# Setup products in borrowed buffers, loads from two queues, and a new order of the late setup work: a two-layer graph network on one Trainium2 core

## The chip, the cores and the metric

The kernel runs on one core of a Trainium2 chip. The core has five engines that run side by side, each with its own queue of instructions in fixed order: TensorE (PE in the profile, with its weight loads as PEld), VectorE (DVE), ScalarE (ACT), GpSimd (POOL) and SyncE (SP), which here only issues DMAs. They wait for one another by semaphores. The metric is the device time of one execution in microseconds, from the first to the last instruction; lower is better.

## The reference

Sixty-four graphs of 256 nodes with 256 features pass through two layers, all in float32. Layer 0 is a graph attention network, layer 1 a transformer layer whose values depend on the kind of edge. Cut to what matters:

```python
def gat(h, adj, W, a):                       # twice, with W1, a1 and W2, a2
    Wh = h @ W
    e = leaky_relu(Wh @ a[:256] + swap(Wh @ a[256:]), 0.2)
    return softmax(where(adj > 0, e, -9e15), axis=1) @ Wh
def layer0(x):
    h = layernorm(x + gat(gat(x, adj, W1, a1), adj, W2, a2))
    return layernorm(h + relu(h @ w_ff1 + b_ff1) @ w_ff2 + b_ff2)
def layer1(s):                               # 8 heads of 32, R = 4 kinds of edge
    attn = softmax(q(s) @ k(s).T / sqrt(32))
    out = sum(attn * (adj == r) @ (s @ Wv[r] + bv[r]) for r in range(4))
    x = layernorm(s + out @ Wo + bo)
    return layernorm(x + gelu(x @ W1 + b1) @ W2 + b2)
```

## The kernel before

**Tiling.** The 64 graphs are taken in 32 pairs. One pair's features are a tile of 128 partitions by 4 by 256. `whole_way(pair)` is the whole course of a pair: `gat_layers` (lines L524, L540 and L553 are its matmuls), `feed_forward` of layer 0 (L677 is its first matrix, in block products of seven instead of eight, L708 its second), `attention` (L750 and L755 make queries, keys and values, L792 scores, L821 and L824 products with the values and the sums, L843 the output matrix), and `feed_forward` of layer 1. Matmul operands are float32; the trace shows each matmul as two records.

**Setup.** Ahead of all pairs, the kernel multiplies the two attention weight matrices of layer 0 together with the vectors `a1` and `a2` into one constant `w12` of 128 x 2 x 260. Four VectorE instructions (L111) form weighted row sums, four matmuls (L117) multiply, and two copies (L119) move the product out of PSUM. Its inputs lie in a pool `setup` of their own, which is closed afterwards; the pools `work` and `psum` are opened after it in the same memory. Adjacency of the first two pairs is loaded into a tile `v` of the pool `work`.

**Reliefs and block sums.** Some biases are folded into residuals, so other constants have to be corrected once. The generator `reliefs()` does it: narrow matmuls with one output column (L908) and a wide pair (L917) on TensorE, small subtractions on VectorE (L910, L919), and `block_sums` (L336), differences of quarters of a weight matrix that the block products need. A pair's first `feed_forward` waits for `relieved[0]`, its attention for `relieved[1]`, its last `feed_forward` for `relieved[2]`.

**The order.** The order of every engine's queue is made when the program is built, by a small planner (`run`, `put`). It keeps a clock for each engine, starting at `START`, and a due time for each event; the landing times of the constant loads are entered by hand (`landed`, `load(0, 11.0)`). Pieces of work for VectorE, ScalarE, GpSimd and SyncE are taken when they are ready, the lowest `rank` first. On TensorE, up to three pairs and the reliefs are generators that yield steps. Of the steps ready for at least `SLACK` microseconds it takes the first by a key; if none is ready for so long, the earliest. The order is then fixed on each engine: an instruction that waits holds up everything behind it on its engine. Two lines carry it:

```python
sure = [n for at, n in times if at <= now - SLACK]
g = going[min(sure, key=lambda n: ("ff" in (going[n][2] or ()) or alone.get("ff") is going[n][0], n))
```

The constant loads are issued by SyncE one after another. A load also waits until the load eight before it has landed, since eight semaphores are used in turn.

Of the kernel before, what the change touches and what calls it, by code (L numbers as in the profile page):

```python
# [10 lines left out]
F32 = mybir.dt.float32  # L11
# [4 lines left out]
ALU = mybir.AluOpType  # L16
AX = mybir.AxisListType

P = 128
# [5 lines left out]
SHIFT = 40.0  # L25
EVEN = 1e-37
HURRIED = 2
SLACK = 0.5
START = {"tensor": 12.0, "vector": 11.0, "scalar": 12.0, "gpsimd": 0.0, "sync": 40.0}


@with_exitstack
def two_layers(ctx: ExitStack, tc: tile.TileContext, t: dict, out: bass.AP, flag: bass.AP):
# [12 lines left out]
    nc = tc.nc  # L46
    B, N, D = out.shape
    NPAIR = B // 2
    KC = D // P
# [46 lines left out]
        nc.sync.dma_start(s, t[name])  # L96
        return s

    w12 = const.tile([P, KC, D + 4], F32, name="w12")
    with tc.tile_pool(name="setup", bufs=1) as setup, \
            tc.tile_pool(name="psetup", bufs=2, space=bass.MemoryType.PSUM) as psetup:
        w1T, a2 = weights("L0_gnn_W1T", setup), on_all("L0_gnn_a2", 2 * D, setup)
        right = setup.tile([P, KC, D + 4], F32, name="right")
        nc.sync.dma_start(right[:, :, :D], t["L0_gnn_W2"].rearrange("(c p) m -> p c m", p=P))
        nc.sync.dma_start(right[:, :, D + 2:], t["L0_gnn_a1c"])
        junk = setup.tile([P, D], F32, name="junk")
        for s in range(2):
            for c in range(KC):  # L110
                nc.vector.scalar_tensor_tensor(  # L111
                    junk, right[:, c, :D], 1.0, a2[:, s * D:(s + 1) * D], op0=ALU.mult, op1=ALU.mult,
                    accum_out=right[:, c, D + s:D + s + 1])
        for m in range(KC):
            pw = psetup.tile([P, 512], F32, name="pw")
            for c in range(KC):
                nc.tensor.matmul(pw[:, :D + 4], lhsT=w1T[:, c, m * P:(m + 1) * P], rhs=right[:, c],  # L117
                                 start=c == 0, stop=c == KC - 1)
            nc.vector.tensor_copy(w12[:, m], pw[:, :D + 4])  # L119
# [4 lines left out]

    def bank():
        return psum.tile([P, 512], F32, name="ps")

# [58 lines left out]
    def at_time(us):  # L186
        event = Event()
        event.time = us
        return event
# [19 lines left out]
    def run(besides, ways, together):  # L209
# [5 lines left out]
        while True:  # L215
# [22 lines left out]
            clock[engine] = now  # L238
            if engine == "tensor":
                sure = [n for at, n in times if at <= now - SLACK]  # L240
                g = going[min(sure, key=lambda n: ("ff" in (going[n][2] or ()) or alone.get("ff") is going[n][0], n))
                          if sure else min(times)[1]]
                alone.update((name, g[0]) for name in g[2] or ())
                takes("bank", g[3])
                for needs in g[4:]:
                    takes(needs)
                step = next(g[0], None)
                if step is None:
                    together -= g[0] is besides
# [235 lines left out]
    def gat_weights(y, at, at_home, ratio, there, to, b):  # L485
# [18 lines left out]
                k = 2 * b + j  # L504
                nc.scalar.activation(y[:, k, :at], y[:, k, :at], AF.Copy, scale=of["rs"][:, j:j + 1])
# [890 lines left out]
```

## Time and profile before

| | before |
|---|---|
| time, three runs | 3067.23, 3071.6 and 3072.2 us, median 3071.6 us |
| the profiled execution | 3069.0 us, span 3067.2 us |
| TensorE busy | 3008.9 us of the span, 98% |
| VectorE, ScalarE, GpSimd busy | 2565.5, 1805.6, 251.5 us |
| mean granted clock of TensorE | 0.991 of full speed |
| DMA | 205.75 MB, mean 67 GB/s |

In the first 80 us TensorE is busy for 60.42 us, in the 2900 us after that for all but some 20 us, and in the last 67.2 us for 48.43 us. All constants, 8 MB and more with the first pairs, come in over the first 50 us; from 20 to 30 us and from 46 to 53 us the DMA engines move about 350 GB/s. The granted clock of TensorE is half of full speed in several stretches of the first 70 us and again from about 3022 to 3031 us.

### The profile page before, as it was taken

How to read it: one execution, taken by the hardware profiler on the slowest of the kernel's cores; microseconds unless marked ns; L12 is line 12 of the kernel's file. 1: busy time of each engine (PE TensorE's matmuls, PEld its weight loads, DVE VectorE, ACT ScalarE, POOL GpSimd, SP SyncE). 2: the span in 40 equal slices, each digit the busy share in tenths (PEclk: the TensorE clock that was granted, in tenths of full speed). 3: DMA queues.
4: the chain of work that ended last, by engine and by line, in shares of the span. 5: the costliest groups of instructions: out<-in, count | busy, mean ns of one | idle time of the engine just before them, and what ended most of it. 6: DMA issues, size and time to landing. Idle time of an engine off the chain costs nothing. (4 is left out here: it accounts for less than half of the span.)

```text
span 3067.2 us, 52833 instructions
## 1 busy us (share of the span) xinstructions
PE 3008.9 (98%) x19138; PEld 2461.4 (80%) x19138; DVE 2565.5 (84%) x5993; ACT 1805.6 (59%) x4124; POOL 251.5 (8%) x518
## 2 busy tenths in 40 slices
PE   7999999999999999999999999999999999999997
PEld 6887778877888888888878888878888878888876
DVE  5798988789888898889798879898878898888875
ACT  3655666556565565665565665565755555755564
POOL 0000000100000001000011000011000010000000
PEclk7999999999999999999999999999999999999998
DMA  5211221211212221221221221221221211221000
GB/s 174 76 56 35 84 95 58 66 59 50 85 56 80 63 76 51 91 73 63 63 77 49 88 79 59 66 73 52 80 87 59 66 62 64 77 83 52 32 6 17
DMA packets 211146, 205.75 MB, mean 67 GB/s; under 512 B 22336, under 2 KB 170432, under 8 KB 210880
## 3 DMA queue, kind: packets, MB, share of 16 engines
q1 hardware_dynamic: 210880, 202.32, 20.7%
q8 instruction: 153, 2.51, 0.3%
q14 instruction: 113, 0.93, 0.1%
HBM read 137.51 MB, written 64.73 MB: 66 GB/s over the span
## 5 line engine op out<-in xcount | busy, mean ns | idle before, releaser
L708 PE MATMUL ps<-w_L_gnn_W,ff 128*128 128x256 f32 x2048 | 464.2, 380 | 2.5 <-ACT ff L689 2.5
L708 PE MATMUL ps<-w_L_gnn_w_ff,ff 128*128 128x256 f32 x2048 | 465.1, 380 | 0.0
L589 ACT ACTIVATE x<-x,less,rstd 128x256 f32<-128x256 f32 x512 | 278.1, 593 | 317.4 <-POOL less L585 316.8
L708 PEld LDWEIGHTS ps<-w_L_gnn_W,ff 128*128 128x128 f32 x2048 | 387.4, 190 | 61.0 <-ACT ff L689 4.3
L708 PEld LDWEIGHTS ps<-w_L_gnn_w_ff,ff 128*128 128x128 f32 x2048 | 387.1, 190 | 59.7 <-issue 6.6
L584 POOL TENSOR_TENSOR rstd<-rstd,mhalf 128x2 f32<-128x2 f32 x256 | 192.1, 750 | 2787.3 <-DVE less L581 2604.1
L803 DVE TENSOR_TENSOR m<-a,adj 128x512 f32<-128x512 f32 x512 | 349.6, 683 | 43.4 <-ACT a L799 43.2
L388 DVE TENSOR_TENSOR ff<-ps,ff 128x512 f32<-128x512 f32 x384 | 259.1, 682 | 91.3 <-PE ps L677 77.0
L677 PE MATMUL ps<-yT,w_L_gnn_W1p 128*128 128x256 f32 x1280 | 314.3, 385 | 12.8 <-ACT ff L683 6.6
L799 ACT ACTIVATE a<-ps 128x512 f32<-128x512 f32 x512 | 268.0, 602 | 97.2 <-PE ps L792 96.3
L677 PE MATMUL ps<-yT,w_L_gnn_w_ff1p 128*128 128x256 f32 x1280 | 307.9, 381 | 1.4 <-ACT ff L683 0.7
L683 ACT ACTIVATE ff<-ps 128x512 f32<-128x512 f32 x384 | 223.0, 590 | 123.6 <-PE ps L677 121.8
L677 PEld LDWEIGHTS ps<-yT,w_L_gnn_W1p 128*128 128x128 f32 x1280 | 240.1, 191 | 61.3 <-ACT ff L683 13.1
L677 PEld LDWEIGHTS ps<-yT,w_L_gnn_w_ff1p 128*128 128x128 f32 x1280 | 241.2, 190 | 42.2 <-ACT ff L683 6.2
L833 DVE RECIPROCAL h<-ps 128x256 f32<-128x256 f32 x128 | 222.6, 1746 | 44.7 <-PE ps L824 44.2
L566 DVE TENSOR_TENSOR x<-ps,x 128x512 f32<-128x512 f32 x256 | 170.6, 680 | 61.4 <-PE ps L708 46.6
L765 ACT ACTIVATE qk<-ps,bqk 128x256 f32<-128x256 f32 x256 | 107.0, 469 | 189.5 <-PE ps L750 189.5
L807 DVE TENSOR_TENSOR h<-a 128x256 f32<-128x256 f32 x512 | 213.5, 417 | 0.0
L578 DVE BATCH_NORM_STATS2 st<-x 128x6 f32<-128x256 f32 x512 | 207.9, 406 | 2.8
L689 ACT ACTIVATE ff<-ff,c_L_gnn_b_ff 128x256 f32<-128x256 f32 x384 | 173.8, 504 | 45.1 <-DVE ff L388 44.5
L689 ACT ACTIVATE ff<-ff,c_L_gnn_b 128x256 f32<-128x256 f32 x384 | 170.4, 502 | 40.9 <-DVE ff L388 39.6
L750 PE MATMUL ps<-yTa,wqk 128*128 128x256 f32 x640 | 167.7, 384 | 0.0
(128 smaller groups left out, 5021.1 us busy)
## 6 DMA issues: line engine op xcount, KB each, us to landing
home<-yb SPq DMA_DIRECT2D x182, 256.0 KB, 2.0
yT<-home SPq DMA_DIRECT2D x728, 64.0 KB, 2.0
rows<-row SPq DMA_DIRECT2D x60, 512.0 KB, 3.9
input<-in_xT SPq DMA_DIRECT2D x32, 512.0 KB, 4.6
x<-in_x SPq DMA_DIRECT2D x32, 512.0 KB, 4.4
out<-x SPq DMA_DIRECT2D x32, 512.0 KB, 3.4
input<-in_adjT SPq DMA_DIRECT2D x30, 512.0 KB, 3.8
v<-in_adjT SPq DMA_DIRECT2D x2, 512.0 KB, 6.5
```

The costliest lines, as they stand in the source:

```text
L388: nc.vector.tensor_tensor(self.target(c, h), self.bank[bank], self.target(c, h), ALU.add)
L578: nc.vector.bn_stats(st[:, j, :], rows[j])
L584: nc.gpsimd.tensor_tensor(rstd, rstd, mhalf[:, :2], ALU.pow)
L589: nc.scalar.activation(rows[j], rows[j], AF.Identity, bias=less[:, j:j + 1], scale=rstd[:, j:j + 1])
L677: nc.tensor.matmul(to, lhsT=w1[:, a, (t + slab) * P:(t + slab + 1) * P], rhs=b, **flags)
L683: return put("scalar", 0.5, lambda: nc.scalar.activation(target(c, h), blocks.bank["x"], AF.Copy), event, rank=-1)
L689: evacuated[h][m] = put("scalar", 0.4, lambda m=m, to=to, source=source: nc.scalar.activation(to, source, func, bias=b1[:, m:m + 1]), even ...
L708: nc.tensor.matmul(p2[:, j * D:(j + 1) * D], lhsT=f[m][:, (2 * j + b) * P:(2 * j + b + 1) * P], rhs=w2[:, m, :], start=m == 0, stop=m == N ...
L799: nc.scalar.activation(a[n][o], ps[o], AF.Exp)
L803: nc.vector.tensor_tensor(m[n][o], a[n][o], adj, ALU.mult)
L807: nc.vector.tensor_tensor(h[n][o], a[n][o][:, :N], a[n][o][:, N:], ALU.add)
L833: there = put("vector", 1.68, lambda: nc.vector.reciprocal(s, po[:, N:]), there, rank=0)
```

## The change

The setup no longer has pools of its own. Its inputs lie in buffers that later work uses (`xw`, two of the tiles `a`, one tile `h`), its products in two of the eight PSUM banks. W2 and W1 transposed are issued by SyncE, `a2` and the small `a1c` by ScalarE. The product is split in two: the 256 columns of the weights first, then the 4 columns of the vectors. The planner's `START` times and the landing times are earlier, and `SLACK` goes from 0.5 to 0.3. Among the steps that TensorE may take, the reliefs come behind all others. Block sums on VectorE go from rank 0 to rank 5, and the attention weights of a pair's second graph from rank 0 to 0.5. What the changed kernel computes is the same.

```diff
-SLACK = 0.5
-START = {"tensor": 12.0, "vector": 11.0, "scalar": 12.0, "gpsimd": 0.0, "sync": 40.0}
+SLACK = 0.3
+START = {"tensor": 8.5, "vector": 8.0, "scalar": 4.0, "gpsimd": 0.0, "sync": 32.0}
...
-    with tc.tile_pool(name="setup", bufs=1) as setup, \
-            tc.tile_pool(name="psetup", bufs=2, space=bass.MemoryType.PSUM) as psetup:
-        w1T, a2 = weights("L0_gnn_W1T", setup), on_all("L0_gnn_a2", 2 * D, setup)
-        right = setup.tile([P, KC, D + 4], F32, name="right")
-        nc.sync.dma_start(right[:, :, :D], t["L0_gnn_W2"].rearrange("(c p) m -> p c m", p=P))
-        nc.sync.dma_start(right[:, :, D + 2:], t["L0_gnn_a1c"])
-        junk = setup.tile([P, D], F32, name="junk")
...
-        for m in range(KC):
-            pw = psetup.tile([P, 512], F32, name="pw")
-            for c in range(KC):
-                nc.tensor.matmul(pw[:, :D + 4], lhsT=w1T[:, c, m * P:(m + 1) * P], rhs=right[:, c],
-                                 start=c == 0, stop=c == KC - 1)
-            nc.vector.tensor_copy(w12[:, m], pw[:, :D + 4])
...
+    right = work.tile([P, 4, D + 4], F32, name="xw", bufs=2)[:, :KC]
+    a2, w1T = (work.tile([P, 512], F32, name="a", bufs=2 * HQ) for _ in range(2))
+    junk = work.tile([P, N], F32, name="h", bufs=2 * HQ)
+    w1T = w1T.rearrange("p (c m) -> p c m", c=KC)
+    nc.sync.dma_start(right[:, :, :D], t["L0_gnn_W2"].rearrange("(c p) m -> p c m", p=P))
+    nc.scalar.dma_start(a2, bass.AP(tensor=t["L0_gnn_a2"].tensor, offset=t["L0_gnn_a2"].offset, ap=[[0, P], [1, 2 * D]]))
+    nc.sync.dma_start(w1T, t["L0_gnn_W1T"].rearrange("(c p) m -> p c m", p=P))
+    nc.scalar.dma_start(right[:, :, D + 2:], t["L0_gnn_a1c"])
...
+    both = [bank() for _ in range(KC)]
+    for columns in (slice(0, D), slice(D, D + 4)):
+        for m in range(KC):
+            for c in range(KC):
+                nc.tensor.matmul(both[m][:, columns], lhsT=w1T[:, c, m * P:(m + 1) * P], rhs=right[:, c, columns],
+                                 start=c == 0 and columns.start == 0, stop=c == KC - 1, skip_group_check=True)
+    for m in range(KC):
+        nc.vector.tensor_copy(w12[:, m], both[m][:, :D + 4])
...
-                g = going[min(sure, key=lambda n: ("ff" in (going[n][2] or ()) or alone.get("ff") is going[n][0], n))
+                g = going[min(sure, key=lambda n: (going[n][0] is besides, "ff" in (going[n][2] or ()) or alone.get("ff") is going[n][0], n))
...
-                        there, rank=0)
+                        there, rank=5)
...
-        there = put("vector", 1.03, lambda: weigh(0), *there, rank=0, needs="e")
-        there = put("vector", 1.11, lambda: weigh(1), there, rank=0, frees=["rows"] * b)
+        there = put("vector", 1.03, lambda: weigh(0), *there, rank=b / 2, needs="e")
+        there = put("vector", 1.11, lambda: weigh(1), there, rank=b / 2, frees=["rows"] * b)
...
-    landed = {name: at_time(us) for name, us in (("ln0", 14.0), ("ff0", 23.0), ("attention", 38.0), ("ff1", 45.0))}
-    loaded = {0: load(0, 11.0)}
+    landed = {name: at_time(us) for name, us in (("ln0", 8.0), ("ff0", 15.0), ("attention", 30.0), ("ff1", 37.0))}
+    loaded = {0: load(0, 6.5)}
...
-    loaded[1] = load(1, 26.0)
+    loaded[1] = load(1, 18.0)
```

More of the change, by code (lines that the diff above doesn't have):

```diff
@@ L97, in column @@
         return s
-    w12 = const.tile([P, KC, D + 4], F32, name="w12")
-    with tc.tile_pool(name="setup", bufs=1) as setup, \
-            tc.tile_pool(name="psetup", bufs=2, space=bass.MemoryType.PSUM) as psetup:
-        w1T, a2 = weights("L0_gnn_W1T", setup), on_all("L0_gnn_a2", 2 * D, setup)
-        right = setup.tile([P, KC, D + 4], F32, name="right")
-        nc.sync.dma_start(right[:, :, :D], t["L0_gnn_W2"].rearrange("(c p) m -> p c m", p=P))
-        nc.sync.dma_start(right[:, :, D + 2:], t["L0_gnn_a1c"])
-        junk = setup.tile([P, D], F32, name="junk")
-        for s in range(2):
-            for c in range(KC):
-                nc.vector.scalar_tensor_tensor(
-                    junk, right[:, c, :D], 1.0, a2[:, s * D:(s + 1) * D], op0=ALU.mult, op1=ALU.mult,
-                    accum_out=right[:, c, D + s:D + s + 1])
-        for m in range(KC):
-            pw = psetup.tile([P, 512], F32, name="pw")
-            for c in range(KC):
-                nc.tensor.matmul(pw[:, :D + 4], lhsT=w1T[:, c, m * P:(m + 1) * P], rhs=right[:, c],
-                                 start=c == 0, stop=c == KC - 1)
-            nc.vector.tensor_copy(w12[:, m], pw[:, :D + 4])
     work = ctx.enter_context(tc.tile_pool(name="work", bufs=1))
@@ L126, in bank @@
         return psum.tile([P, 512], F32, name="ps")
+    w12 = const.tile([P, KC, D + 4], F32, name="w12")
+    right = work.tile([P, 4, D + 4], F32, name="xw", bufs=2)[:, :KC]
[6 more added lines that the diff above has]
+    nc.scalar.dma_start(right[:, :, D + 2:], t["L0_gnn_a1c"])
+    for s in range(2):
+        for c in range(KC):
+            nc.vector.scalar_tensor_tensor(
+                junk, right[:, c, :D], 1.0, a2[:, s * D:(s + 1) * D], op0=ALU.mult, op1=ALU.mult,
+                accum_out=right[:, c, D + s:D + s + 1])
+    both = [bank() for _ in range(KC)]
+    for columns in (slice(0, D), slice(D, D + 4)):
+        for m in range(KC):
+            for c in range(KC):
+                nc.tensor.matmul(both[m][:, columns], lhsT=w1T[:, c, m * P:(m + 1) * P], rhs=right[:, c, columns],
+                                 start=c == 0 and columns.start == 0, stop=c == KC - 1, skip_group_check=True)
+    for m in range(KC):
+        nc.vector.tensor_copy(w12[:, m], both[m][:, :D + 4])
     engines = {"tensor": mybir.EngineType.PE, "vector": mybir.EngineType.DVE, "scalar": mybir.EngineType.Activation,
```

## The prediction

> **What bounds the kernel now.** I read the page's busy times and slices first, then TensorE's waits in three stretches, then the timeline of the first 80 us and of the end.
>
> ```profile
> PE 3008.9 (98%) x19138; PEld 2461.4 (80%) x19138; DVE 2565.5 (84%) x5993; ACT 1805.6 (59%) x4124; POOL 251.5 (8%) x518
> ...
> PE   7999999999999999999999999999999999999997
> ...
> PEclk7999999999999999999999999999999999999998
> ```
>
> TensorE is busy 98% of the time. It is idle, or at a lower granted clock, in the first and the last slice only. The change removes no work from TensorE: what it can win is idle time and half-clock time. Idle is 3067.2 - 3008.9 = 58.3 us: 19.6 us before 80 us, 18.8 us after 3000 us (7.8 us of it between matmuls, 10.9 us behind the last one), and about 20 us between.
>
> ```profile
> 11.13 0.37 SPq L287 DMA_DIRECT2D v<-in_adjT  x1
> ...
> 11.62 3.77 PE L524 MATMUL ps<-w,input 128*128 128x260 f32 x16 [0.52 <-DVE w L119]
> ...
> 15.55 1.28 ACT L299 ACT_TABLE_LOAD   x1 [15.55 <-DMA v<-in_adjT]
> ...
> 19.48 1.94 PE L460 MATMUL ps<-ident,rise 128*128 128x128 f32 x8 [4.09 <-ACT rise L447]
> ...
> 28.68 6.62 PE L540 MATMUL ps<-xw,e 128*128 128x258 f32 x16
> ...
> 43.57 5.41 PE L553 MATMUL ps<-xw,e 128*128 128x256 f32 x16 [3.89 <-ACT xw L505]
> ...
> 45.55 0.43 DVE L895 TENSOR_TENSOR b_L_gnn_beta<-b_L_gnn_beta,ff 128x256 f32<-128x256 f32 x1 [1.13 <-DMA b_L_gnn_beta<-in_L_gnn_beta]
> ...
> 63.25 6.42 PE L540 MATMUL ps<-xw,e 128*128 128x258 f32 x16 [2.90 <-ACT xw L505]
> ```
>
> The adjacency load waits until 11.13 us for the setup's memory; SyncE's waits name L111, L117 and the setup's loads. ScalarE stands at it until 15.55 us, and behind it in its queue stand the copies that release TensorE at 19.48 us. L540 takes 6.62 us at half clock, against 1.90 + 2.01 us for the same matmuls at 94 us.
>
> ```profile
> PE ps L677 <- ACT ff L683: 9.5, 11, 2.2
> PE ps L677 <- DMA yT<-home: 3.6, 1, 3.6
> PE ps L708 <- ACT ff L689: 2.5, 2, 1.6
> ```
>
> These are the longest waits of TensorE between 80 and 3011 us, nearly all before 940 us; later one wait of 1.17 us returns every 463 us. Last, the end:
>
> ```profile
> 3014.90 1.96 PE L843 MATMUL ps<-w_L_gnn_Wo,qk 128*128 128x256 f32 x8
> 3022.69 1.94 PE L645 MATMUL ps<-ident,x 128*32 128x128 f32 x32 [5.83 <-DVE x L594]
> 3025.93 1.94 PE L645 MATMUL ps<-ident,x 128*32 128x128 f32 x32 [1.30 <-DVE x L594]
> 3028.57 4.27 PE L677 MATMUL ps<-yT,w_L_gnn_W1p 128*128 128x256 f32 x12 [0.71 <-ACT yT L649]
> ```
>
> The last pair's layer norm has no other pair's matmuls beside it, and the matmuls after it run at half clock.
>
> **What the Trainium skill says.** "TensorE: Matmul & The Clock Gate", Part 1 (The HAM clock gate), has the PE at half clock after an idle window of about 3.4 us and at full clock after such a busy one. The trace agrees in kind: 0.50 granted after the gaps of 4.09, 3.89 and 5.83 us. It also drops to 0.50 near 55 us with TensorE busy, behind 32 one-column records of L908. "Trainium Kernel Development and Optimization", Key Constraints, says that DMAs from several queues share the same 16 engines, so a second queue only saves issue time. The trace has about 0.45 us per issue on SyncE.
>
> **The start, part by part.** *Setup.* The four loads of 768 KB landed by 6.2 us in the old kernel. In the new one the same bytes come by the same engines, the two that L111's successor needs first of all: I take 5.0 us (bounds 4.3 and 6.2), with W1 transposed at 6.0. The four row sums are hidden under the split matmuls: eight records of 256 columns at the old half-clock pace (3.53 us for eight) end at 9.5. The four narrow matmuls are new, eight records at 0.11 to 0.22 us as in L908: 0.9 to 1.8 us. Two copies of 0.43 us follow, partly under them. `w12` is ready at about 11, against 11.57: a gain of 0 to 2 us only.
>
> *Adjacency.* With no pool to wait for, SyncE issues it at about 2.3 us. About 1.8 MB lie up to its end; at the old rates (1.14 MB by 6.0 us, then 0.35 MB/us) it lands at 8.2, not 15.5. ScalarE: 8.2 + 1.28 + 1.06 = 10.5, so the copies follow the matmuls. First L524 group 11.2 to 15.0, copies and exponentials as before (0.4 + 0.3), L460 at about 15.7: 3.8 us earlier, with an idle gap too short to lower the clock.
>
> *First relief and L540.* L908 keeps its place: 32 records at 0.11 us, 16.7 to 20.2; its weights land by 14. The old L460 to L505 time (19.48 to 24.12) gives L505 at 20.3, but the second adjacency copy now stands ahead of it on ScalarE and lands at 19.9 (1.5 MB behind a backlog), so L505 is free at 21. L540 runs 21.5 to 28.1 if at half clock again, against 35.3 before.
>
> *The new wait.* VectorE's queue now has the subtraction on the layer-1 beta (old L895) and one on `wv` ahead of the second attention weights; before, they came behind. Beta lands late because it is the 44th load. The second adjacency's x landed at 30.2 in the old kernel and at about 21.3 by the same rates in the new; the next 22 loads are issue-bound in both, so beta comes at 45.5 - 8.9 = 36.6 (bounds 34 and 39). The weights then start at 36.6 + 0.43 + 0.38 = 37.4 instead of about 32.8, TensorE idles some 8 us, and L553 starts at 37.4 + 3.75 = 41.1, 2.5 us before 43.57. Behind the stalled VectorE queue stand L505 and L553, nothing else.
>
> *Reliefs behind the rest.* Then the row transposes of pair 1 (L460) go ahead of L908, L917 and L908, whose 7.8 us cover the weights that TensorE waited 2.90 us for at 63.25. L540 starts at about 55.5; counting L645, which now follows it, the lead is about 6 us. Block sums at rank 5 are hidden: VectorE is idle for some 36 of the first 80 us. **Start: 5.5 us won, bounds 0 and 11.**
>
> **The middle.** The order of the changed program differs from the old nearly everywhere, so this was read from the order itself. From the 2,300th to the 8,956th of 9,588 matmuls the new TensorE order repeats every 292, one pair, some 23 times (the old order repeats every 1,460, five pairs). So a wait in it counts 23 times. I walked one period with the old durations (0.43 us per 256-column matmul, L683 0.59, L799 0.52, L803 with L807 0.93). The block products are interleaved with attention, and every wait has over 0.4 us to spare but one: the copy of the first product of the last feed-forward ends about 0.1 to 0.2 us after TensorE could use it, behind three exponentials. That is 0.2 x 23 = 4.6 us, bounds 0 and 14. For the stretch before the period I take 9 us, from 13.5 us of waits in the old one up to 940 us, bounds 5 and 15. Together 13.6, against 20.1. **Middle: 6 us won, bounds -9 and +15.**
>
> **The end.** The new order leaves 16 matmuls of the previous pair (two groups of 8 x 0.43 = 3.45 us) between the last L843 and the last block products; before, all were done earlier. The layer-norm chain to L645 is as long as before, so L677 again starts some 11.7 us after L843 ends, but with 6.9 us of work done in it, and the clock need not fall (L677 4.27 to 2.75, L645 1.94 to 1.0). **End: 7 us won, bounds 3 and 10.**
>
> Sum against the profile's own span: 3067.2 - 5.5 - 6 - 7 = 3048.7. The three runs are 3067.2 to 3072.2 with a median of 3071.6; between the span and the median I predict 3052.
>
> **Rivals.** *A: as summed*, 3052, its own range 3044 to 3062. *B: the setup wins nothing*: loads share the engines, beta lands at 39, the middle is as before, and only the end gains about 5: 3062 by the span, 3066 on the scale of the runs. For it: DMA at 350 GB/s from 20 us on, and the late beta. Against it: two idle stretches of the DMA queue, 3.5 to 11.1 us, are simply removed. *C: slower.* A wait sits in the repeated period on the chain L677 to L683 to L677. It decides from (5.5 + 7 + 20.1 - 9) / 23 = 1.03 us per pair; at 1.64 us, the second longest such ScalarE wait before, it is 38 us, and the time 3067.2 - 12.5 + (9 + 38 - 20.1) = 3081.6 by the span, 3085 on the scale of the runs. For it: a smaller `SLACK` and one period for all. Against: products interleaved, and the old period of five lost only 2.5 us per 463. *D: better.* Beta lands by 34 and the period has no wait: start 9, middle 12, end 9: 3037 by the span, 3041 on the scale of the runs.
>
> **Numbers.** A 0.62, D 0.19, B 0.11, C 0.08. Below 0.2% (about 6 us) a measurement here can't tell a change from none. Faster takes A, D and a part of B: 0.84; same 0.08; slower 0.08. The range takes A and D and B's near side: 3037 to 3067.
>
> **What would show it.** Right: L299 before 11 us, the subtraction on beta at about 37 with VectorE idle before it, L553 near 41, no L540 wait near 60, matmuls of the old L708 between the last L645 groups. Wrong: one wait of over 1 us on L677 repeated some 23 times, or L553 later than 43.6.

## The result, and the profile after

| | before | after |
|---|---|---|
| time, median of 4 runs each | 3071.38 us (3067.23 to 3072.2) | 3046.14 us (3044.99 to 3049.07) |
| ratio, with its 95% interval | | 0.9922 [0.9905, 0.9939] |
| the same kernel in a later comparison | 3070.40 us (9 runs) | 3040.97 us (4 runs), 0.9908 [0.9893, 0.9923] |
| profiled execution: span, mean clock | 3067.2 us, 0.991 | 3047.2 us, 0.995 |

The change makes the kernel faster by some 25 to 29 us. The forecast was 3052, within 3037 to 3067. The profiled execution of the changed kernel was the slowest of its four (3049.07 us), so its trace accounts for 20.0 us of that. Busy times and slices on the page of the changed kernel:

```profile
PE 2996.3 (98%) x19146; PEld 2452.5 (80%) x19146; DVE 2556.8 (84%) x5993; ACT 1752.5 (58%) x4096; POOL 252.6 (8%) x518
...
PE   7999999999999999999999999999999999999998
...
PEclk8999999999999999999999999999999999999999
```

TensorE's busy time fell by 12.6 us though its work is nearly the same: that is time at half clock. Its idle time fell by 7.4 us. The timeline of the start (start, duration, engine and line, tiles, and in brackets the idle time before and what ended it):

```profile
2.25 0.47 SPq L291 DMA_DIRECT2D v<-in_adjT  x1
...
7.46 4.64 PE L127 MATMUL ps<-xw,a 128*128 128x256 f32 x16 [7.46 <-DMA a<-in_L_gnn_W1T]
10.08 1.06 ACT L303 ACTIVATE adj<-v 128x1024 uint8<-128x1024 int32 x1 [6.91 <-DMA v<-in_adjT]
...
16.87 1.06 PE L464 MATMUL ps<-ident,rise 128*128 128x128 f32 x8 [0.90 <-ACT rise L451]
...
23.38 1.06 ACT L303 ACTIVATE adj<-v 128x1024 uint8<-128x1024 int32 x1 [4.86 <-DMA v<-in_adjT]
...
24.90 5.45 PE L544 MATMUL ps<-xw,e 128*128 128x258 f32 x16 [3.50 <-ACT xw L509]
...
39.65 0.43 DVE L899 TENSOR_TENSOR b_L_gnn_beta<-b_L_gnn_beta,ff 128x256 f32<-128x256 f32 x1 [4.84 <-DMA b_L_gnn_beta<-in_L_gnn_beta]
...
43.98 6.11 PE L557 MATMUL ps<-xw,e 128*128 128x256 f32 x16 [9.26 <-ACT xw L509]
...
57.81 5.41 PE L544 MATMUL ps<-xw,e 128*128 128x258 f32 x16
```

(Lines have moved by four: L464 was L460, L544 was L540, L557 was L553, L681 was L677, L712 was L708, L847 was L843.) The adjacency is issued at 2.25 us, and TensorE goes on at 16.87 instead of 19.48 us with 0.90 instead of 4.09 us of waiting. Then the second adjacency holds ScalarE until 23.38 us, and beta holds VectorE until 39.65, so L557 starts at 43.98 us, 0.4 us later than before, after a wait of 9.26 us. The second group L544 has no wait. The first product of L681 starts at 69.80 us, before at 75.10. The timeline of the end:

```profile
2996.46 1.89 PE L847 MATMUL ps<-w_L_gnn_Wo,qk 128*128 128x256 f32 x8
2998.18 3.62 PE L712 MATMUL ps<-w_L_gnn_W,ff 128*128 128x256 f32 x16
3001.78 1.08 PE L649 MATMUL ps<-ident,x 128*32 128x128 f32 x32
3002.79 3.72 PE L712 MATMUL ps<-w_L_gnn_W,ff 128*128 128x256 f32 x16
3007.20 1.08 PE L649 MATMUL ps<-ident,x 128*32 128x128 f32 x32 [0.69 <-DVE x L598]
3008.99 2.86 PE L681 MATMUL ps<-yT,w_L_gnn_W1p 128*128 128x256 f32 x12 [0.71 <-ACT yT L653]
```

Two groups L712 of the pair before stand in the layer norm of the last pair. The wait of 5.83 us is gone, and L681 takes 2.86 instead of 4.27 us. From the end of the last L847 to the end of the span it is 48.85 us, before 50.34; 6.9 us of L712 now lie inside it, so the end has gained 1.5 + 6.9 = 8.4 us. With 5.3 us at the first L681 product and a difference of 20.0 between the spans, 6.3 us are left for what lies between. In the trace of the later comparison, with a span of 3039.2 us, the same reckoning gives 5.7 us at the start, 8.5 at the end and 13.8 between: the two ends agree, the middle does not.

### The profile page after: what moved, and what is told of

It reads as the page before. It is cut to its first block, busy times and chain, and to the rows that moved or that the text cites. A ratio compares the mean times of both kernels' runs of the same rounds, so it can differ in the third digit from the quotient of the medians.

```text
span 3047.2 us, 52870 instructions
## 1 busy us (share of the span) xinstructions
PE 2996.3 (98%) x19146; PEld 2452.5 (80%) x19146; DVE 2556.8 (84%) x5993; ACT 1752.5 (58%) x4096; POOL 252.6 (8%) x518
## 4 chain that ended last, share of the span: by engine, by line
PE 63%; DVE 25%; DMA 6%; ACT 2%; SPq 1%; issue 1%; POOL 0%; DVEq 0%; ACTq 0%; POOLq 0%
PE ps L712 21%; PE ps L681 15%; PE ps L825 5%; DVE x L598 4%; PE ps L759 4%; PE ps L754 4%; PE ps L544 3%; DVE h L837 3%; PE ps L796 3%; DMA home<-yb 3%; DVE st L582 2%; DVE m L807 2%; PE ps L557 2%; DMA rows<-row 2%; DVE ff L392 2%; PE ps L847 2%
## 5 line engine op out<-in xcount | busy, mean ns | idle before, releaser
L712 PE MATMUL ps<-w_L_gnn_w_ff,ff 128*128 128x256 f32 x2048 | 470.9, 381 | 0.0
L712 PE MATMUL ps<-w_L_gnn_W,ff 128*128 128x256 f32 x2048 | 456.1, 380 | 1.8 <-ACT ff L693 1.8
L712 PEld LDWEIGHTS ps<-w_L_gnn_w_ff,ff 128*128 128x128 f32 x2048 | 386.6, 190 | 61.5 <-issue 9.8
L712 PEld LDWEIGHTS ps<-w_L_gnn_W,ff 128*128 128x128 f32 x2048 | 388.2, 190 | 57.6 <-ACT ff L693 2.6
L588 POOL TENSOR_TENSOR rstd<-rstd,mhalf 128x2 f32<-128x2 f32 x256 | 198.3, 775 | 2765.7 <-DVE less L585 2638.0
L807 DVE TENSOR_TENSOR m<-a,adj 128x512 f32<-128x512 f32 x512 | 350.1, 684 | 57.9 <-ACT a L803 57.8
L681 PE MATMUL ps<-yT,w_L_gnn_W1p 128*128 128x256 f32 x1280 | 315.2, 382 | 4.7 <-ACT ff L687 2.4
L392 DVE TENSOR_TENSOR ff<-ps,ff 128x512 f32<-128x512 f32 x384 | 262.7, 685 | 66.4 <-PE ps L681 58.3
L681 PE MATMUL ps<-yT,w_L_gnn_w_ff1p 128*128 128x256 f32 x1280 | 308.8, 382 | 6.8 <-ACT ff L687 5.9
L681 PEld LDWEIGHTS ps<-yT,w_L_gnn_w_ff1p 128*128 128x128 f32 x1280 | 240.6, 190 | 50.8 <-ACT ff L687 18.8
L687 ACT ACTIVATE ff<-ps 128x512 f32<-128x512 f32 x384 | 223.9, 590 | 98.4 <-PE ps L681 97.6
L681 PEld LDWEIGHTS ps<-yT,w_L_gnn_W1p 128*128 128x128 f32 x1280 | 240.2, 190 | 48.2 <-ACT ps L835 8.5
L837 DVE RECIPROCAL h<-ps 128x256 f32<-128x256 f32 x128 | 223.4, 1746 | 21.3 <-PE ps L828 20.9
L509 ACT ACTIVATE xw<-xw,rs 128x258 f32<-128x258 f32 (+1 forms) x256 | 115.9, 502 | 200.7 <-DVE rs L504 200.6
L693 ACT ACTIVATE ff<-ff,c_L_gnn_b_ff 128x256 f32<-128x256 f32 x384 | 171.6, 504 | 97.4 <-DVE ff L392 97.0
L693 ACT ACTIVATE ff<-ff,c_L_gnn_b 128x256 f32<-128x256 f32 x384 | 173.3, 501 | 85.0 <-DVE ff L392 83.8
L570 DVE TENSOR_TENSOR x<-ps,x 128x512 f32<-128x512 f32 x256 | 170.2, 682 | 16.4 <-PE ps L712 9.3
```

The lines of the kernel that those rows point to most:

```text
L392: nc.vector.tensor_tensor(self.target(c, h), self.bank[bank], self.target(c, h), ALU.add)
L588: nc.gpsimd.tensor_tensor(rstd, rstd, mhalf[:, :2], ALU.pow)
L681: nc.tensor.matmul(to, lhsT=w1[:, a, (t + slab) * P:(t + slab + 1) * P], rhs=b, **flags)
L687: return put("scalar", 0.5, lambda: nc.scalar.activation(target(c, h), blocks.bank["x"], AF.Copy), event, rank=-1)
L693: evacuated[h][m] = put("scalar", 0.4, lambda m=m, to=to, source=source: nc.scalar.activation(to, source, func, bias=b1[:, m:m + 1]), even ...
L712: nc.tensor.matmul(p2[:, j * D:(j + 1) * D], lhsT=f[m][:, (2 * j + b) * P:(2 * j + b + 1) * P], rhs=w2[:, m, :], start=m == 0, stop=m == N ...
```

## The experiments

All twelve kernels were timed in five rounds, four to a comparison; the kernel before took 3070.17, 3070.47 and 3070.40 us in the three. Each of the three ran on a chip of its own; which chip the result above came from is not on record. Idle time of TensorE is read from the busy times by stretch, 80 to 1000 us and 1000 to 2900 us. "Fill" says whether L712 products stand between the last L847 and the last L649.

| kernel | time, us | ratio, 95% | idle 80-1000 | idle 1000-2900 | fill |
|---|---|---|---|---|---|
| before | 3070 to 3071 | 1 | 14.3 | 5.5 | no |
| after, first comparison | 3046.14 | 0.9905 to 0.9939 | 6.5 | 7.2 | yes |
| 1: setup alone | 3066.75 | 0.9980 to 0.9997 | 17.3 | 5.8 | no |
| 1: planner's numbers alone | 3045.81 | 0.9907 to 0.9934 | 6.5 | 2.4 | yes |
| 1: later landings | 3053.75 | 0.9935 to 0.9963 | 7.6 | 4.8 | yes |
| 1: `SLACK` undone | 3055.19 | 0.9936 to 0.9963 | 16.4 | 0.1 | no |
| 2: `SLACK` and attention rank alone | 3048.38 | 0.9919 to 0.9946 | 6.2 | 1.5 | yes |
| 2: attention rank alone | 3050.09 | 0.9922 to 0.9949 | 7.5 | 0.1 | no |
| 2: all loads from SyncE | 3042.05 | 0.9892 to 0.9922 | 6.7 | 4.1 | yes |
| 2: longer lag for the rows | 3053.99 | 0.9937 to 0.9965 | 5.0 | 11.8 | yes |
| 3: after, again | 3040.97 | 0.9893 to 0.9923 | 6.0 | 2.7 | yes |
| 3: reliefs' key undone | 3049.49 | 0.9925 to 0.9952 | 6.2 | 2.7 | yes |
| 3: numbers alone, two queues | 3042.45 | 0.9899 to 0.9926 | 6.0 | 0.4 | yes |
| 3: all loads from SyncE, again | 3041.09 | 0.9894 to 0.9925 | 6.1 | 4.5 | yes |

### Setup or numbers

The change has two halves: the setup in borrowed buffers, and the planner's numbers. The first kernel is the changed one with all numbers of before.

```diff
-SLACK = 0.3
+SLACK = 0.5
...
-    landed = {name: at_time(us) for name, us in (("ln0", 8.0), ("ff0", 15.0), ("attention", 30.0), ("ff1", 37.0))}
+    landed = {name: at_time(us) for name, us in (("ln0", 14.0), ("ff0", 23.0), ("attention", 38.0), ("ff1", 45.0))}
```

(and likewise `START`, the loads' times, the key and the ranks). What was expected:

> New setup (borrowed buffers, two load queues), all planner numbers and so the whole order of work as in the kernel before. Theory: the start is one part of the gain, the order of the middle and the end the rest. The adjacency then lands near 10 us, and without the wait on beta the start gains 5 to 7 us: about 3065 us. Rival: the setup is worth nothing without the new order (the product w12 is no earlier): within 2 us of before, 3070.

It took 3066.75 us, 3.4 less than before: less of a gain than the theory's 5 to 7 us, and more than the rival's 2. Its first product of the first feed-forward starts at 69.03 us, 6.1 us earlier than before. Set side by side along the same order of TensorE, that lead is 4.9 to 7.4 us from 83 to 830 us and 2.4 us when the middle ends.

The second has the old setup, with its pools, and all new numbers:

```diff
-    right = work.tile([P, 4, D + 4], F32, name="xw", bufs=2)[:, :KC]
-    a2, w1T = (work.tile([P, 512], F32, name="a", bufs=2 * HQ) for _ in range(2))
+    with tc.tile_pool(name="setup", bufs=1) as setup, \
+            tc.tile_pool(name="psetup", bufs=2, space=bass.MemoryType.PSUM) as psetup:
+        w1T, a2 = weights("L0_gnn_W1T", setup), on_all("L0_gnn_a2", 2 * D, setup)
...
```

> Old setup with its own pools, all planner numbers and so the whole order of work as in the changed kernel. Theory: the end gains 8 us and the middle 6 us as in the changed kernel, but beta lands at 45.5 us as before and the wait on it costs some 6 us of that: about 3061 us, 15 us above the changed kernel. Rival: the order is worth nothing, all the gain is the setup's: 3070 or more.

It took 3045.81 us. My theory had asked for 3061: it held that the start is worth its 5 us to the end, and it fell. The planner's numbers alone bring nearly the whole gain. The first feed-forward product starts at 75.59 us, no earlier than before. The lines of that product, with the setup alone and with the numbers alone:

```profile
69.03 2.75 PE L683 MATMUL ps<-yT,w_L_gnn_w_ff1p 128*128 128x256 f32 x12
```

```profile
75.59 2.75 PE L675 MATMUL ps<-yT,w_L_gnn_w_ff1p 128*128 128x256 f32 x12
```

That comparison had no run of the changed kernel, so a third kernel was run beside it: the old setup and new numbers once more, with `a2` and `a1c` issued by ScalarE. Every instruction but those of the setup then stands on each engine as in the changed kernel.

```diff
-        w1T, a2 = weights("L0_gnn_W1T", setup), on_all("L0_gnn_a2", 2 * D, setup)
+        w1T, a2 = weights("L0_gnn_W1T", setup), setup.tile([P, 2 * D], F32, name="b_L0_gnn_a2")
+        nc.scalar.dma_start(a2, bass.AP(tensor=t["L0_gnn_a2"].tensor, offset=t["L0_gnn_a2"].offset, ap=[[0, P], [1, 2 * D]]))
...
-        nc.sync.dma_start(right[:, :, D + 2:], t["L0_gnn_a1c"])
+        nc.scalar.dma_start(right[:, :, D + 2:], t["L0_gnn_a1c"])
```

> The old setup with all new numbers, as in the earlier run of 3045.8, but with the loads of a2 and a1c issued by ScalarE; all orders are those of that run but for these two loads. Theory (a second queue that has once been used makes the later transfers a little slower): 3048 to 3051, VectorE's waits for the rows up from 35 us to 42 or more. Rival (the queue has no later effect): 3044 to 3047, waits as before.

3042.45 us, against 3040.97 for the changed kernel on the same chip: 1.5 us, which these runs can't tell from none. Yet at the same matmul the changed kernel leads by 6.8 to 7.2 us from 80 to 830 us. The lead shrinks to 4.7 us by 1430 and to 1.5 us by 2930. So two pairs of runs agree: of the new setup's 6 to 7 us at the start, 1.5 to 3.4 us reach the end. (The first traces of the changed kernel and of the numbers alone come from two comparisons; there a lead of 5.8 us at 80 us has become a lag of 2.4 us by 2930.) The theory of this run, that a used second queue slows later transfers, fell too, and the time lies 1.6 us below its rival's range; more on that below.

### Which number carries it

The next kernel is the one before with a single change:

```diff
-        there = put("vector", 1.03, lambda: weigh(0), *there, rank=0, needs="e")
-        there = put("vector", 1.11, lambda: weigh(1), there, rank=0, frees=["rows"] * b)
+        there = put("vector", 1.03, lambda: weigh(0), *there, rank=b / 2, needs="e")
+        there = put("vector", 1.11, lambda: weigh(1), there, rank=b / 2, frees=["rows"] * b)
```

> The kernel before with only the rank b / 2 of the attention weights on VectorE; SLACK stays at 0.5. Its order has the period of one pair but no matmul of the previous pair between the last Wo product and the last block products. Theory (end and middle each carry a part): 8.5 us of the end are missing, about 3055, within 3051 to 3059. Rival 1 (the period of one pair carries all): 3046 to 3049. Rival 2 (the tail carries all): 3066 to 3070.

3050.09 us: between the theory's 3051 to 3059 and the first rival's 3046 to 3049. This one rank brings 20.4 us. TensorE's order has the period of one pair, and its idle time from 80 to 2900 us falls from 19.8 to 7.6 us; after 745 us it waits for 0.2 us in all before the end. These waits are 12.3 of the 18.9 us between the two profiled executions; the rest isn't broken down. The changed kernel with this rank alone undone was not run. The groups of TensorE's waits from 80 to 2990 us, of this kernel (totals, times, longest; the line numbers are those of before):

```profile
PE ps L677 <- ACT ff L683: 2.2, 4, 0.7
PE ps L821 <- DVE m L803: 1.6, 5, 0.3
PE ps L540 <- ACT xw L505: 1.0, 1, 1.0
```

L677 behind L683 had 9.5 us before, and the wait of 3.6 us for `yT` is gone. The end is that of before, which the timeline of this kernel shows:

```profile
2994.89 1.97 PE L843 MATMUL ps<-w_L_gnn_Wo,qk 128*128 128x256 f32 x8
3002.69 1.94 PE L645 MATMUL ps<-ident,x 128*32 128x128 f32 x32 [5.84 <-DVE x L594]
3005.93 1.94 PE L645 MATMUL ps<-ident,x 128*32 128x128 f32 x32 [1.30 <-DVE x L594]
```

With `SLACK` at 0.3 as well (`-SLACK = 0.5`, `+SLACK = 0.3`) the 16 products stand at the end:

> The kernel before with only two of the planner's numbers of the change: SLACK 0.3, and b / 2 as the rank of the attention weights on VectorE. The setup, the ranks of the block sums, the key that sends the reliefs behind the rest, START and the landing times are those of before. Its TensorE order has the period of one pair and the 16 matmuls of the previous pair between the last Wo product and the last block products; its last 8,706 records stand in the same order as in the run with the old setup and all new numbers. Theory (the tail and the period carry the gain, the start is worth nothing): as that run, 3046, within 3042 to 3050. Rival 1 (the start's numbers count after all: reliefs behind the rest, later loads expected): 3051 to 3056. Rival 2 (the gain needs all numbers): 3065 or more.

3048.38 us, inside the theory's range. But it is only 1.7 us below the run with the rank alone, not 8.5, and the intervals overlap. The fill is no free gain: after 745 us this kernel waits 4.8 us ahead of its last output matrix, against 0.2. Of that 3.0 us fall between 2908 and 2986 us, in four waits that every kernel with the fill has in the same place. At the end it gains 9.7 us on the rank alone; the waits take back 4.6, and what takes the rest isn't broken down.

The reverse, the changed kernel with `SLACK` back at 0.5:

> Changed kernel with SLACK back at 0.5. The order is the same over the first 43 rows of TensorE's queue, repeats one pair as well, but at the end no matmuls of the previous pair are left between the last output matrix and the last transposes. Theory: the end loses 8 us, the middle stays: about 3054 us. Rival: the smaller SLACK is what shortened the middle too, so 14 us or more are lost: 3060. Second rival: SLACK does nothing: 3046.

3055.19 us, near the theory's 3054, in part by luck. The end has its gaps of 5.84, 1.30 and 0.71 us again. But the middle did not stay as it was: from 1000 to 2900 us this kernel waits 0.1 us, and new waits are early, 3.37 us at 248 us and 4.09 us for `yT` at 313 us, so that the idle time of 80 to 1000 us is 16.4 us. `SLACK` decides the order of the first thousand microseconds as much as the end.

### The reliefs' key

The changed kernel without the new key:

```diff
-                g = going[min(sure, key=lambda n: (going[n][0] is besides, "ff" in (going[n][2] or ()) or alone.get("ff") is going[n][0], n))
+                g = going[min(sure, key=lambda n: ("ff" in (going[n][2] or ()) or alone.get("ff") is going[n][0], n))
```

> The changed kernel without the new key, so that the biases' reliefs keep their place by age among the streams of TensorE. The order is the same from the first attention stream on, apart from four products, and so is the end; between 40 and 140 us the reliefs stand inside L557, ahead of the transposes of pair 1. Theory (the reliefs of 7.4 us hid the wait for the weights of L544, 3 us before): TensorE waits again at its second L544, 2 to 4 us, of which the middle gives a part back: 3047 to 3050. Rival (they are put into L557's wait instead, which needs filling too): 3043 to 3046.

3049.49 us, 8.5 us more than the changed kernel on the same chip, with intervals that don't meet. That is at the upper end of the theory's 3047 to 3050; the rival fell. Its timeline shows more than a wait that comes back:

```profile
44.84 3.78 PE L557 MATMUL ps<-xw,e 128*128 128x256 f32 x8 [8.94 <-ACT xw L509]
48.41 3.41 PE L912 MATMUL ps<-c_L_gnn_boc,wqk 128*128 128x1 f32 x16
51.69 3.76 PE L921 MATMUL ps<-wv,c_L_gnn_boc 128*128 128x256 f32 x8
55.24 6.83 PE L912 MATMUL ps<-c_L_gnn_b2c,w_L_gnn_W1p 128*128 128x1 f32 x32
61.93 3.76 PE L557 MATMUL ps<-xw,e 128*128 128x256 f32 x8
...
72.40 3.81 PE L544 MATMUL ps<-xw,e 128*128 128x258 f32 x8 [3.90 <-ACT xw L509]
```

The reliefs take 14.0 us here, each at its half-clock pace: 16 narrow records 3.41 us, against 1.84 at full clock in the changed kernel. There they come behind all 16 records of L557, which have brought the clock up by then, and they need 7.4 us. TensorE is busy from 44.84 to 68 us here, and the granted clock is 0.50 from 40 to 60 us. Then the weights are late all the same, 3.90 us. The changed kernel in the same comparison:

```profile
43.87 5.88 PE L557 MATMUL ps<-xw,e 128*128 128x256 f32 x16 [9.95 <-ACT xw L509]
...
50.45 1.84 PE L912 MATMUL ps<-c_L_gnn_boc,wqk 128*128 128x1 f32 x16
...
57.46 5.41 PE L544 MATMUL ps<-xw,e 128*128 128x258 f32 x16
```

The profiled execution without the key was the slowest of its five, at 3056.53 us. From 160 us on both orders are the same; there it is 14.5 us behind the trace of the changed kernel, and at the end 15.5 us. This lag was not made up. But only two of the five executions are like that, with 3056 us and a mean granted clock of 0.992. The other three took 3048.08 to 3049.49 us at 0.994 to 0.995, near the changed kernel's 0.995 to 0.996, so most of the added half clock is not in them. How the 8.5 us of the medians divide into clock and waits stays open.

The reliefs can lower the clock in their new place too: L544 behind them takes 5.41 us in this trace of the changed kernel. With all loads from SyncE, in the same comparison and the same order, it takes 3.73 us, at a granted clock of 1.00 from 55 to 61 us.

### The landing times

The trace after shows VectorE standing 4.84 us for beta. So the planner was told that the attention constants land later:

```diff
-    landed = {name: at_time(us) for name, us in (("ln0", 8.0), ("ff0", 15.0), ("attention", 30.0), ("ff1", 37.0))}
+    landed = {name: at_time(us) for name, us in (("ln0", 8.0), ("ff0", 15.0), ("attention", 39.5), ("ff1", 46.5))}
```

> Changed kernel with the planner's landing times of the attention and last feed-forward weights set to what the trace shows (39.5 and 46.5 us). The order differs over the first 250 rows of TensorE's queue and is the same from there to the end, so only the start is tried. Theory: the subtraction on beta goes behind the attention weights, L557 starts near 36 instead of 44 us, and 3 to 7 us are won: about 3042 us. Rival: the next late load (the third adjacency at 48.6 us, or the reliefs' weights) takes the wait's place: 3046, no change.

3053.75 us, slower than the changed kernel. Theory and rival both missed the time, though the rival had named the load that takes the wait's place. VectorE no longer waits for beta, and L557 starts at 40.21 us with a wait of 4.26 us. But the reliefs, which wait for the same constants, come only at 68 us. From the timeline of this kernel:

```profile
48.47 1.06 ACT L303 ACTIVATE adj<-input 128x1024 uint8<-128x1024 int32 x1 [6.81 <-DMA input<-in_adjT]
49.44 1.19 ACT L467 ACTIVATE rows<-ps 128x256 f32<-128x256 f32 x4
...
55.40 6.27 PE L544 MATMUL ps<-xw,e 128*128 128x258 f32 x16 [9.01 <-ACT xw L509]
```

ScalarE stands 6.81 us at the third adjacency, and the exponentials L467 behind it are what L544 waits for. In the changed kernel ScalarE stands there too, until 48.60, but the late L557 and the reliefs lie in that time. One wait was taken away and another, 9.01 us long, took its place. The first L681 product starts 2 us late (71.77 against 69.80), and 32 narrow records of the reliefs are still to come behind it. From 434 us on both orders are the same, and there this kernel lies some 9 us behind the first trace of the changed kernel. By the end it is 3.6 us behind, since that trace loses more in the middle; behind the changed kernel's second trace it is 9.7 us at 500 us and 11.6 at the end.

### Why the lead is given back

In the new period VectorE waits once in nearly every pair for `rows`, the spread of an attention row to all partitions by DMA (512 KB). VectorE's waits from 80 to 2990 us (totals, times, longest), in the changed kernel and in the one before:

```profile
DVE e L499 <- DMA rows<-row: 44.8, 24, 3.9
```

```profile
DVE e L495 <- DMA rows<-row: 9.3, 12, 2.7
```

Most cost TensorE nothing. At 1114 us the timeline of the changed kernel shows one that does:

```profile
1109.24 0.51 SPq L482 DMA_DIRECT2D rows<-row  x1
...
1114.54 0.48 DVE L499 SCALAR_TENSOR_TENSOR e<-rows,ratio 128x256 f32<-128x256 f32 x1 [2.42 <-DMA rows<-row]
...
1116.79 0.91 ACT L693 ACTIVATE ff<-ff,c_L_gnn_b_ff 128x256 f32<-128x256 f32 x2 [2.18 <-DVE ff L392]
1117.61 0.58 ACT L687 ACTIVATE ff<-ps 128x512 f32<-128x512 f32 x1
...
1118.23 1.13 PE L681 MATMUL ps<-yT,w_L_gnn_w_ff1p 128*128 128x256 f32 x4 [1.05 <-ACT ff L687]
```

Read it downwards: the rows land 5.3 us after their issue; VectorE, in order, stands 2.42 us; its sum L392 comes late; ScalarE stands at L693 for it; the copy L687 behind L693 comes late; TensorE waits 1.05 us. At the same place the run with the numbers alone had 4.3 us from issue to landing:

```profile
1118.17 0.48 DVE L493 SCALAR_TENSOR_TENSOR e<-rows,ratio 128x256 f32<-128x256 f32 x1 [0.71 <-DMA rows<-row]
...
1120.42 0.91 ACT L687 ACTIVATE ff<-ff,c_L_gnn_b_ff 128x256 f32<-128x256 f32 x2 [0.46 <-DVE ff L386]
```

A wait of 0.71 us is lost in the slack of the queues. Matmul by matmul along the same order, the changed kernel loses time against that run at waits alone: from 1130 to 2780 us, some 5 us at 20 to 25 places with a gap, some 1 us at small steps around them, and nothing at the other 10,400 or so records. Against the kernel with the old setup in the third comparison it is the same from 1000 to 2900 us: 4.1 us at gaps and 1.2 us around them. Not each of these waits was followed back to the rows.

Two theories of why the changed kernel waits more were tried. The first: the second queue. All four loads from SyncE, with the order of everything later the same:

```diff
-    nc.scalar.dma_start(a2, bass.AP(tensor=t["L0_gnn_a2"].tensor, offset=t["L0_gnn_a2"].offset, ap=[[0, P], [1, 2 * D]]))
+    nc.sync.dma_start(a2, bass.AP(tensor=t["L0_gnn_a2"].tensor, offset=t["L0_gnn_a2"].offset, ap=[[0, P], [1, 2 * D]]))
...
-    nc.scalar.dma_start(right[:, :, D + 2:], t["L0_gnn_a1c"])
+    nc.sync.dma_start(right[:, :, D + 2:], t["L0_gnn_a1c"])
```

> The changed kernel with all four loads of the setup issued by SyncE; the order of everything later is the same. SyncE issues two more loads at 0.45 us each ahead of W1 and of the first adjacency, so w12 comes later by up to 0.9 us and the first adjacency too. Theory (a lead at the start is given back in the middle, where VectorE waits for the spread of the attention rows once per pair): the same as the changed kernel, 3046, within 3043 to 3049, and the profile again shows some 24 waits of VectorE for rows of 35 to 45 us in all. Rival 1 (the start counts one to one): 3047 to 3048, not to be told from theory. Rival 2 (the second queue is what disturbs the later transfers): the waits for rows fall to well below 35 us and the time to 3040 or less.

3042.05 us, 1 us below the theory's range and 4 us less than the changed kernel in its own comparison; that looked like an effect of the queue, though VectorE's waits for the rows, 38.6 us, had not fallen as the second rival asked. So both were run on one chip:

> The changed kernel once more, on the chip of this comparison, as the partner of the one-queue kernel and of the kernels below. Theory (the second queue costs about 4 us later on): 3046, within 3044 to 3049, some 4 us above the one-queue kernel of the same comparison, and again 40 us or more of VectorE's waits for the rows. Rival (chance of one placement or chip): 3042 to 3046, within 1.5 us of the one-queue kernel.

> The changed kernel with all loads of the setup from SyncE once more, on the same chip as the changed kernel. Theory: 3042, within 3040 to 3044, 3 to 5 us below the changed kernel. Rival: 3043 to 3047, within 1.5 us of it.

3040.97 and 3041.09 us: no difference that these runs could show. The rival was right in that, though both times lie 1 to 2 us below its ranges. The changed kernel itself was 5 us faster than in the first comparison. Its new trace has TensorE's waits from 1000 to 2900 us as follows:

```profile
PE ps L754 <- ACT qk L769: 1.1, 4, 0.5
PE ps L681 <- ACT ff L687: 1.0, 3, 0.7
```

and in the first comparison:

```profile
PE ps L681 <- ACT ff L687: 5.1, 9, 1.4
PE ps L754 <- ACT qk L769: 1.3, 3, 0.8
```

The adjacency loads, which SyncE issues ahead of the rows, took a mean of 4.4 us from issue to landing in this trace and 4.5 us in the first, and VectorE's waits for the rows were 37.1 and 44.8 us. This fits one explanation, that a period with so little slack behind the rows turns small delays of transfers into waits. It is not shown by a change of the transfers alone, and one pair speaks against it: the numbers alone, with one queue and with two, had the same mean of 4.4 us and waits for the rows of 35.3 and 35.1 us, and took 3045.81 and 3042.45 us in two comparisons.

The second theory: if the rows are what matters, the planner should expect them later.

```diff
-        return at_home, ratio, [put("sync", 0.4, spread, there, rank=0, lag=2.5, kb=512, needs="rows")]
+        return at_home, ratio, [put("sync", 0.4, spread, there, rank=0, lag=3.0, kb=512, needs="rows")]
```

> The changed kernel with one number more changed: the planner expects the spread of an attention row to land 3.0 instead of 2.5 us after its transfer. Its order is that of the changed kernel in the first matmuls, then a longer period of eight pairs, with the 16 matmuls at the end kept. Theory (VectorE's once-a-pair wait for the rows, 24 waits of 44.8 us in the changed kernel, is what makes TensorE wait in the middle): the waits for rows fall to 25 us or less, the waits of TensorE between 940 and 2900 us from 6.3 to 3 us or less, and the time to 3040 to 3044. Rival (any new order of the middle brings waits of its own): the waits for rows fall, but others come, 3046 to 3053.

3053.99 us. The waits for the rows fall to 11.0 us in 8 places, but the period of eight pairs that the planner makes of it has waits of its own: 11.8 us from 1000 to 2900 us, on VectorE's sums L392 and ScalarE's copies. The rival was right in kind, 1 us above its range. The start of this kernel was earlier than that of the changed kernel (first L681 product at 67.98 against 69.80 us), and that did not make up for the new waits.

What stays open is why the changed kernel waits more than the run with the old setup on the same chip, in the same order: 2.7 against 0.4 us of idle time from 1000 to 2900 us, with waits for the rows of 37.1 and 35.1 us and the same mean landing time of the adjacency, 4.4 us. No run changed that alone.

## Why the prediction was right, point by point

The time, 3046.14 against 3052, lies 5.9 us below the forecast and near the middle of its range. Its three terms, against the span: start 5.5 forecast and 5.3 measured, middle 6 and 6.3, end 7 and 8.4. That all three fit is in part luck. The middle is a remainder, and in the later trace it is 13.8 us. In the two runs of the numbers alone, which have no lead at the start, it is 14.5 and 19.0 us. So the middle's own gain was more than twice the forecast, and giving the start back in it hid that.

*Setup, "a gain of 0 to 2 us only".* Too hopeful. I took the first loads to land at 5.0 us, within 4.3 to 6.2; `W2` landed at 6.65 and W1 transposed at 7.33. The first use of the product began at 12.18 us, 0.6 us later than before, and at 11.59 in the later trace, no earlier than before (11.62). The second queue made this worse: the setup's first matmul started at 6.76 to 7.46 us in the seven traces of the new setup with two queues, and at 6.32 and 6.39 in the two with one, 0.7 and 0.5 us ahead of a kernel with two in the same comparison.

*Adjacency.* Issued at 2.25 us as forecast (2.3), landed at 10.06, not 8.2 (by the forecast's own figures, 1.14 MB by 6.0 us and then 0.35 MB/us up to 1.8 MB, 7.9). The mechanism held, since ScalarE's copy was still ready before the matmuls behind it; L464 came 2.6 us earlier, not 3.8.

*First relief and L540.* The wait for the second adjacency was forecast at 19.9 us and lasted until 23.4, so the weighted matmuls started at 24.90, not 21.5. They took 5.45 us, not 6.6.

*The new wait on beta.* The mechanism was right to the line: VectorE idle, the subtraction, then L509 and L557. The size was not. I had beta landing at 36.6 us, within 34 to 39, and it landed at 39.56. The term that failed was the time of the second adjacency's `x`, 21.3 in the estimate and 24.70 in the trace, on which the rest of the loads follows. L557 started at 43.98, not 41.1, and by the test that I had set ("later than 43.6") this step was wrong.

*Reliefs behind the rest.* Right: L912, L921 and L912 fill 50.8 to 57.9 us, and L544 has no wait. I counted it as a wait of 2.90 us saved. The run without the key puts it at 8.5 us; in its profiled execution the reliefs also ran at half clock, for 14.0 instead of 7.4 us. That what the late beta cost came back here, so that the start was 5.3 us, was luck.

*The start as a gain.* Here the prediction's reasoning failed, though not its sum. It added the start to the end as if TensorE carried a lead through. Of 6 to 7 us at 80 us, the setup keeps 1.5 to 3.4.

*The middle.* I expected 13.6 us of waits, of which 4.6 in one repeated wait of 0.2 us, the copy of L681 behind three exponentials. That wait isn't there. I had walked the period with durations of instructions, and found everything else 0.4 us to spare. What the walk left out is that a transfer has no fixed duration: from 80 to 2990 us of the first trace, the rows landed 3.3 to 6.5 us after their issue. Measured: 6.5 + 7.2 us up to 2900 us and 3.0 us after, 16.7 in all, in the first trace; 6.0 + 2.7 + 3.0 = 11.7 in the second. With 20.0 before, waits make 3.3 us of the 6.3 and 8.3 of the 13.8; the rest isn't broken down (the clock from 80 to 400 us, 0.99 before and 1.00 after, is a part of it).

*The end.* Right: the 16 products, the two groups, L681 at 2.86 (forecast 2.75), L649 at 1.08 (1.0). The forecast of 7 was for the end alone. It missed that the fill must be taken from somewhere: 3.0 us of waits between 2909 and 2987 us, which I had looked for only in the period.

Rival B (setup worth nothing, 3066) was right about the loads and the beta and wrong about the sum. Rival C (a wait of over 1.03 us in each pair) has a relative in the traces, irregular and through VectorE and the rows, of 7.2 us in all from 1000 to 2900 us instead of 38. (The loss of the old period, put at 2.5 us per 463 against C, is 1.3 in the trace.) D (3041) is where the later comparison landed, without its reasons: beta did not land by 34 us.

What no part of the prediction saw is the size of one number. The rank of the attention weights alone makes the period of one pair and 20 us; I had read that the period was there, and priced the whole middle at 6 us, since the waits that I counted before came to 20.1 and I put 13.6 in the new order.

## What to carry to other kernels

In a kernel with one full engine and in-order queues, a lead at the start is not yet time won: follow it, matmul by matmul, through the steady part, and price first the number that sets the order of the repeated part. A lag can stay whole, as the 14.5 us of the run without the key did. When walking such a period, give each transfer a spread of landing times, not one; a wait of VectorE that costs nothing in most pairs can still cost TensorE time in some. Run two kernels in one comparison before explaining 4 us in 3000, look at every execution's clock before giving a profiled one for the median, and try narrow matmuls behind wide ones that have already raised the clock.

## What the hardware showed that was not expected

- Narrow matmuls did not raise TensorE's clock in the profiled execution without the key. TensorE was busy from 44.84 to 68 us, and the clock was 0.50 from 40 to 60 us and 0.65 from 60 to 80. "TensorE: Matmul & The Clock Gate", Part 1, in the Trainium skill has full clock after a busy window of about 3.4 us. With wide matmuls this case agrees: the 16 records of L557 in the changed kernel took 5.88 us in its second trace, less than twice the 3.78 us of eight at half clock, and the reliefs behind them ran at full clock. By the trace's busy time it doesn't where one-column records stand between stretches of 3.8 us of wide ones: there the half clock held for more than 20 us. Not every execution was like that. An estimate from the mean clocks (twice the missing share, times the span) gives some 49 us at half clock in all in the profiled one, at 0.992, and 30 to 37 us in the three of the five at 0.994 to 0.995. What decides is open.
- The same changed kernel took 3046.14 us in one comparison and 3040.97 in another, while the kernel before took 3071.38 and 3070.40. Up to 830 us its two traces keep within 0.7 us of each other; the rest of the 8 us between their spans is lost later, with 7.2 against 2.7 us of idle time from 1000 to 2900 us. Whether the chip or the transfers cause it isn't shown.
- Two queues for the first four loads made no difference that could be measured in the time (3040.97 and 3041.09 us), and brought the last of the setup's inputs 0.5 and 0.7 us later in the two comparisons that had both. "Trainium Kernel Development and Optimization", Key Constraints, in the Trainium skill has several queues share the same 16 engines; these runs agree.
